# Attention with the keys on the partitions: no transposes, no row maximum, a range check behind a branch

## The chip, the cores and the metric

The kernel runs on one core of one Trainium2 chip. PE is its matmul engine, an array of 128 rows by 128 columns; DVE is the vector engine, ACT the scalar engine (here exp and tanh), POOL a general engine. PSUM is the memory that the PE writes. The metric is the device time of one execution in microseconds (us). Ratios are the mean time of one kernel's fast runs over that of the other's fast runs of the same rounds, so they are not quite the ratio of the medians that I quote.

One caution holds for all ratios of the experiments: in their rounds the kernel before ran mostly at two levels, near 4247 us (granted clock 0.985) and near 4267 to 4270 us (0.980 to 0.981), with a few runs between, all counted as fast. This widens the intervals to plus or minus 0.3 to 0.4%. The variants themselves repeat within 4 us, so I compare the variants' own medians, and read from the trace where the microseconds lie. The changed kernel was not run again on the chips of the experiments, and the two levels lie 20 us apart, so a difference of up to some 20 us alone proves nothing without its line in the trace.

## The reference, cut to what matters

Eight images of 512 channels and 32 x 32 pixels go through GroupNorm, a C2f-style block with two attention bottlenecks, and a residual add, all in float32. One bottleneck is a 3x3 convolution, the attention below (4 heads of 64 channels, 1024 pixels), and a 1x1 convolution ("m2") with silu and a residual. So the attention runs sixteen times.

```python
def bot_attention(x, qkv_w, rw, rh):
    b, c, h, w = x.shape
    hw = h * w                                        # 1024
    qkv = conv2d(x, qkv_w, 0).reshape(b, 3, HEADS, HD, hw)
    q, k, v = (qkv[:, 0], qkv[:, 1], qkv[:, 2])
    r = (rw + rh).reshape(1, HEADS, HD, hw)
    logits = jnp.einsum('bhdi,bhdj->bhij', q, k + r) * HD ** (-0.5)
    a = jax.nn.softmax(logits, axis=-1)
    out = jnp.einsum('bhij,bhdj->bhdi', a, v)
    return out.reshape(b, c, h, w)
```

## The kernel before

Channels lie on the partitions, pixels along the free axis. A pair of heads (128 channels) is worked on together: head 0 has rows 0 to 63 of the PE, head 1 rows 64 to 127. For 128 queries at a time:

```python
# logits of 128 queries: a PSUM tile for each head
ls = [ps_big.tile([P, NH, HALF], F32, tag="big", name="l_ps") for _ in range(2)]
for half in range(NH):
    for hd in range(2):
        r = slice(hd * HD, (hd + 1) * HD)
        nc.tensor.matmul(ls[hd][:, half, :], q[r, c, i0 : i0 + P], kr[r, c, ts(half, HALF)], ...)
for hd in range(2):
    nc.vector.tensor_reduce(nm, flat, AX.X, ALU.max, negate=True)        # row maximum
    nc.scalar.activation(e, flat, AF.Exp, bias=nm, accum_out=sums[:, ic, hd : hd + 1])
...
# transposes, so that the keys come to the partitions
for j in range(4):
    nc.tensor.transpose(tp[:, j, :], es[hd][:, ts(g + j, P)], ident)
...                                   # tp is copied to pts by DVE or ACT
# the reciprocal of the row sums is brought to the free axis by a product with ident
nc.vector.reciprocal(ri, sums)
nc.gpsimd.tensor_copy(rb, ri.unsqueeze(3).to_broadcast([P, NIC, 2, HD]))
nc.tensor.matmul(ps[:, 1, ts(ic, P)], rb[:, ic]..., ident, ...)
# the product with v: the heads on two halves of the PE's columns
nc.tensor.matmul(ps[hd * HD : (hd + 1) * HD, 0, :], vT[:, j, o : o + HD], pts[hd][:, j, :], ...)
```

Of the kernel before, what the change touches and what calls it, by code (L numbers as in the profile page):

```python
"""GroupNorm -> C2f-style conv block with two attention bottlenecks -> residual add.

Layout: channels on the partitions, the 1024 pixels of one image along the free axis. All of the
weights stay in SBUF; one image at a time goes through the whole block without touching HBM in
between. Everything is float32.

Attention, for a pair of heads (128 channels) and 128 queries at a time: logits with the queries on
the partitions (the two heads use the two halves of the PE rows), the row maximum on VectorE, exp
with its row sum on ScalarE, transposes on the PE, and the product with v^T for 256 queries (the two
heads use the two halves of the PE columns). The division by the row sum follows that product.  # L10

silu(y) = h * (1 + tanh(h)) with h = y / 2, which keeps Exp and Tanh in one activation table.
"""

# [1 line left out]

# [7 lines left out]
F32 = mybir.dt.float32  # L24
AF = mybir.ActivationFunctionType
ALU = mybir.AluOpType
AX = mybir.AxisListType
PSUM = bass.MemoryType.PSUM

# [3 lines left out]
GROUP = 16  # channels per GroupNorm group  # L33
HD = 64


@with_exitstack
def kernel(
    ctx: ExitStack,
    tc: tile.TileContext,  # L40
    x: bass.AP,        # (B, C1, HW)
    cv1_w: bass.AP,    # (C1, 2C)           input channel first
    cv1_bn: bass.AP,   # (2C, 4)
    cv2_w: bass.AP,    # (4C, C2)
    cv2_bn: bass.AP,   # (C2, 4)
    m_cv1_w: bass.AP,  # (N, C, 9, C)       input channel, tap, output channel
    m_cv1_bn: bass.AP,  # (N, C, 4)
    m_qkv_w: bass.AP,  # (N, C, 3C)
    m_rw: bass.AP,     # (N, C, F)
    m_rh: bass.AP,     # (N, C, F)  # L50
    m_cv2_w: bass.AP,  # (N, C, C)
    m_cv2_bn: bass.AP,  # (N, C, 4)
    out: bass.AP,      # (B, C2, HW)
# [6 lines left out]
    NX = C1 // P         # channel chunks of x  # L60
    NM = C // P          # channel chunks (= head pairs) of a bottleneck
    NO = C2 // P
    NJ = HW // P         # key chunks
    HALF = 512           # pixels of one matmul
    NH = HW // HALF
    ROWS = HALF // F
    IB = 256             # queries of one product with v
    NIB = HW // IB
    NIC = IB // P

    const = ctx.enter_context(tc.tile_pool(name="const", bufs=1))
    act = ctx.enter_context(tc.tile_pool(name="act", bufs=1))
    small = ctx.enter_context(tc.tile_pool(name="small", bufs=4))
    ps_big = ctx.enter_context(tc.tile_pool(name="ps_big", bufs=2, space=PSUM))
    ps_tr = ctx.enter_context(tc.tile_pool(name="ps_tr", bufs=2, space=PSUM))
    ps_av = ctx.enter_context(tc.tile_pool(name="ps_av", bufs=2, space=PSUM))

# [1 line left out]
    def load_x(b, c):  # L79
        xt = act.tile([P, HW], F32, tag="x", name=f"x_{b}_{c}", bufs=5)  # L80
        nc.sync.dma_start(xt, x[b, ts(c, P), :])
        return xt

    xs = [load_x(0, c) for c in range(NX)]

# [34 lines left out]
    ident = const.tile([P, P], F32, name="ident")  # L120
    make_identity(nc, ident)
    # gmat averages over the channels of a group and gives each of them the result.
# [14 lines left out]
    # y1 and y2 are kept with a border of zeros, which the 3x3 convolutions read.  # L137
# [10 lines left out]
    # BatchNorm as y/2 = sh * conv + bh: sh = g / sqrt(v + eps) / 2, bh = b / 2 - m * sh  # L148
# [16 lines left out]
    def silu_parts(ps, k):  # L165
        """h = y / 2 and tanh(h), of one PSUM bank; k names the BatchNorm chunk."""
        h = act.tile([P, HALF], F32, tag="h", name="h", bufs=2)
        t = act.tile([P, HALF], F32, tag="t", name="t", bufs=2)
        nc.vector.tensor_scalar(h, ps, sh[:, k : k + 1], bh[:, k : k + 1], ALU.mult, ALU.add)  # L169
        nc.scalar.activation(t, h, AF.Tanh)  # L170
        return h, t

    def silu(dst, ps, k):
        h, t = silu_parts(ps, k)
        if len(dst.shape) == 3:
            h, t = img(h), img(t)
        nc.vector.scalar_tensor_tensor(dst, t, 1.0, h, ALU.add, ALU.mult)

    def conv1x1(w_of, rhs_of, nk):
        """[P, NH, HALF] in PSUM: sum over nk chunks, both halves per weight."""  # L180
        ps = ps_big.tile([P, NH, HALF], F32, tag="big", name="ps")
        for k in range(nk):
            for half in range(NH):
                nc.tensor.matmul(  # L184
                    ps[:, half, :], w_of(k), rhs_of(k, half), start=(k == 0), stop=(k == nk - 1)
                )
        return ps

# [1 line left out]
    def gn_stats(mv, c, xt):  # L190
        st = small.tile([P, NH, 6], F32, tag="st", name="st")
        for half in range(NH):
            nc.vector.bn_stats(st[:, half, :], xt[:, ts(half, HALF)])
        nc.vector.bn_aggr(mv[:, c, :], st.rearrange("p a b -> p (a b)"))

    def gn_mean(mv):
        """Group means; mv's variances become those about the group's mean."""
        ps = ps_av.tile([P, NX], F32, tag="av", name="gm_ps")
        nc.tensor.matmul(ps, gmat, mv[:, :, 0], start=True, stop=True)
        gm = small.tile([P, NX], F32, tag="gm", name="gm")  # L200
        dev = small.tile([P, NX], F32, tag="dev", name="dev")
        nc.vector.tensor_copy(gm, ps)
        nc.vector.tensor_tensor(dev, mv[:, :, 0], gm, ALU.subtract)
        nc.vector.tensor_tensor(dev, dev, dev, ALU.mult)
        nc.vector.tensor_tensor(dev, dev, mv[:, :, 1], ALU.add)
        return gm, dev

    def gn_apply(gm, dev, xts):
        ps = ps_av.tile([P, NX], F32, tag="av", name="gv_ps")
        nc.tensor.matmul(ps, gmat, dev, start=True, stop=True)  # L210
        gr = small.tile([P, NX], F32, tag="gr", name="gr")
        nc.vector.tensor_scalar(gr, ps, GN_EPS, None, ALU.add)
        nc.gpsimd.tensor_tensor(gr, gr, mhalf[:, :NX], ALU.pow)
        xn = []
        for half in range(NH):
            t = act.tile([P, NX, HALF], F32, tag="pt", name="xn", bufs=3)
            for c in range(NX):
                nc.vector.tensor_scalar(  # L218
                    t[:, c, :], xts[c][:, ts(half, HALF)],
                    gm[:, c : c + 1], gr[:, c : c + 1], ALU.subtract, ALU.mult,  # L220
                )
            xn.append(t)
        return xn

# [1 line left out]
    def attention(n, z):  # L226
        q = act.tile([P, NM, HW], F32, tag="q", name="q")
        kr = act.tile([P, NM, HW], F32, tag="k", name="kr")
        vT = act.tile([P, NJ, C], F32, tag="v", name="vT")

        def project(which, c):
            o = which * C + c * P
            return conv1x1(
                lambda k: qkv_sb[:, n, k, o : o + P], lambda k, half: z[:, k, ts(half, HALF)], NM
            )

        def project_qk(c):
            ps = project(0, c)
            for half in range(NH):
                nc.scalar.activation(q[:, c, ts(half, HALF)], ps[:, half, :], AF.Copy, scale=HD**-0.5)  # L240
            ps = project(1, c)
            for half in range(NH):
                dst = img(kr[:, c, ts(half, HALF)])
                rw = rw_sb[:, n, c, :].unsqueeze(1).to_broadcast([P, ROWS, F])
                rh = rh_sb[:, n, c, ts(half, ROWS)].unsqueeze(2).to_broadcast([P, ROWS, F])
                nc.vector.tensor_tensor(dst, img(ps[:, half, :]), rw, ALU.add)  # L246
                nc.vector.tensor_tensor(dst, dst, rh, ALU.add)  # L247

        project_qk(0)
        per = NH * HALF // C  # L250
        for j0 in range(0, NJ, per):
            ps = ps_big.tile([P, per, C], F32, tag="big", name="v_ps")
            for j in range(per):
                for k in range(NM):
                    nc.tensor.matmul(  # L255
                        ps[:, j, :], z[:, k, ts(j0 + j, P)], qkv_sb[:, n, k, 2 * C : 3 * C],
                        start=(k == 0), stop=(k == NM - 1),
                    )
            for g in range(0, per, per // NH):
                nc.scalar.copy(vT[:, j0 + g : j0 + g + per // NH, :], ps[:, g : g + per // NH, :])  # L260
# [219 lines left out]
```

## Time and profile before

| | before |
|---|---|
| median time, 4 runs | 4267.16 us (4266.83 to 4267.4) |
| PE busy | 4025.7 us, 94% |
| attention with m2, mean per image, first and second bottleneck | 133.2 and 136.6 us |
| PE waits of the 3x3 convolutions on DVE | 10.0 us in all |

The prediction below shows the page's main lines. Four rows of the costliest groups are added here. A row reads: line, engine, operation, output and inputs with their sizes, number of records (a pair such as `64*128` is the part of the PE's array that is used, rows by columns); then the busy time in us and the mean of one in ns; then the idle time of the engine before them and what ended it.

```profile
L375 PE MATMUL c_ps<-ypad,m_sb 128*128 128x512 f32 x2304 | 994.8, 593 | 10.0 <-DVE ypad L398 10.0
...
L290 ACT ACTIVATE e<-l_ps,nm 128x1024 f32<-128x1024 f32 x512 | 571.7, 1117 | 629.7 <-DVE nm L288 551.0
L288 DVE TENSOR_REDUCE nm<-l_ps 128x1 f32<-128x1024 f32 x512 | 603.3, 1219 | 358.9 <-PE l_ps L280 358.9
...
L306 DVE COPY pt<-tp 128x512 f32<-128x512 f32 x512 | 351.1, 686 | 228.5 <-PE tp L303 221.2
```

### The profile page before, as it was taken

The numbers are of one execution on the slowest core, as the hardware profiler recorded it, in microseconds if no ns is written. First come the engines' busy times: TensorE is split into PE (matmuls) and PEld (weight loads), VectorE is DVE, ScalarE is ACT, GpSimd is POOL, SyncE is SP. The second block draws the span as 40 slices with busy tenths as digits, with TensorE's granted clock in tenths as the row PEclk, the third lists the DMA queues.
The fourth block names the chain that finished last, engine by engine and source line by source line (L and its number), as shares of the span: only waits on it lengthen the run. The fifth ranks groups of instructions, "written<-read, shape, count | busy, mean of one in ns | idle before, by whom it ended". The sixth has DMA issues, their size and how long they took to land.

```text
span 4268.1 us, 38190 instructions
## 1 busy us (share of the span) xinstructions
PE 4025.7 (94%) x15904; PEld 2044.4 (48%) x15904; DVE 1618.2 (38%) x2252; ACT 1156.4 (27%) x2049; POOL 108.5 (3%) x243
## 2 busy tenths in 40 slices
PE   7999999999999999999999999999999999999998
PEld 3545545445454544545445454454544445444454
DVE  2433424334243442434424244242442424424243
ACT  0323303233042330423204132041420414204142
POOL 1000000000000000000000000000000000000000
PEclk9999999999999999999999999999999999999999
DMA  3000000000000000000100001000010000100000
GB/s 120 1 1 1 17 24 1 1 1 20 20 1 1 1 20 20 1 1 1 30 10 1 1 1 30 10 1 1 1 30 10 1 0 1 35 0 1 1 1 20
DMA packets 14700, 46.12 MB, mean 11 GB/s; under 512 B 3264, under 2 KB 3776, under 8 KB 14016
## 3 DMA queue, kind: packets, MB, share of 16 engines
q1 hardware_dynamic: 4608, 16.78, 1.6%
q0 software_dynamic: 5632, 16.82, 1.0%
q10 hardware_dynamic: 4288, 10.09, 0.6%
q8 instruction: 125, 2.05, 0.2%
q14 instruction: 47, 0.39, 0.0%
HBM read 26.90 MB, written 16.78 MB: 10 GB/s over the span
## 4 chain that ended last, share of the span: by engine, by line
PE 86%; DVE 6%; ACT 4%; issue 3%; DMA 0%; POOL 0%; ACTq 0%; SPq 0%; POOLq 0%; DVEq 0%
PE c_ps L375 23%; PE ps L184 22%; PE l_ps L280 18%; PE av_ps L326 11%; PE tp L303 10%; ACT e L290 4%; DVE nm L288 4%; PE v_ps L255 3%; DVE kr L246 0%; DVE kr L247 0%; DVE h L169 0%; DMA x<-in_x_dram 0%; DVE t L393 0%; DVE t L420 0%; ACT pt L308 0%
## 5 line engine op out<-in xcount | busy, mean ns | idle before, releaser
L375 PE MATMUL c_ps<-ypad,m_sb 128*128 128x512 f32 x2304 | 994.8, 593 | 10.0 <-DVE ypad L398 10.0
L280 PE MATMUL l_ps<-kr,q 64*128 64x512 f32 x2048 | 857.3, 659 | 146.0 <-ACT e L290 146.0
L290 ACT ACTIVATE e<-l_ps,nm 128x1024 f32<-128x1024 f32 x512 | 571.7, 1117 | 629.7 <-DVE nm L288 551.0
L288 DVE TENSOR_REDUCE nm<-l_ps 128x1 f32<-128x1024 f32 x512 | 603.3, 1219 | 358.9 <-PE l_ps L280 358.9
L375 PEld LDWEIGHTS c_ps<-ypad,m_sb 128*128 128x128 f32 x2304 | 434.1, 189 | 569.3 <-issue 546.1
L303 PEld LDWEIGHTS tp<-ident,e 128*128 128x128 f32 x4096 | 448.5, 143 | 419.2 <-issue 211.9
L170 ACT ACTIVATE t<-h 128x512 f32<-128x512 f32 x256 | 161.3, 630 | 1692.9 <-DVE h L169 1682.9
L303 PE MATMUL tp<-ident,e 128*128 128x128 f32 x4096 | 595.7, 284 | 1.4
L326 PE MATMUL av_ps<-pt,vT 128*64 128x256 f32 x4096 | 473.1, 382 | 0.0
L280 PEld LDWEIGHTS l_ps<-kr,q 64*128 64x128 f32 x2048 | 264.3, 193 | 372.5 <-ACT e L290 183.7
L306 DVE COPY pt<-tp 128x512 f32<-128x512 f32 x512 | 351.1, 686 | 228.5 <-PE tp L303 221.2
L326 PEld LDWEIGHTS av_ps<-pt,vT 128*64 128x64 f32 x4096 | 291.7, 137 | 210.8 <-issue 87.6
L169 DVE TENSOR_SCALAR h<-c_ps,sh,bh 128x512 f32<-128x512 f32 x64 | 48.9, 806 | 887.2 <-PE c_ps L375 887.2
L308 ACT COPY pt<-tp 128x512 f32<-128x512 f32 x512 | 297.3, 581 | 295.5 <-PE tp L303 295.5
L169 DVE TENSOR_SCALAR h<-ps,sh,bh 128x512 f32<-128x512 f32 x192 | 148.0, 805 | 338.4 <-PE ps L184 338.4
L184 PE MATMUL ps<-xn,cv_sb 128*128 128x512 f32 x512 | 240.9, 634 | 15.6 <-DVE xn L218 15.6
L184 PE MATMUL ps<-z,qkv_sb 128*128 128x512 f32 x512 | 227.7, 595 | 0.0
L184 PE MATMUL ps<-ypad,cv_sb 128*128 128x512 f32 x512 | 225.9, 592 | 0.0
L332 DVE TENSOR_TENSOR ao<-av_ps,rs 128x256 f32<-128x256 f32 x128 | 54.2, 424 | 347.2 <-ACT rs L331 347.2
L184 PEld LDWEIGHTS ps<-xn,cv_sb 128*128 128x128 f32 x512 | 103.8, 205 | 146.8 <-issue 125.6
L184 PEld LDWEIGHTS ps<-ypad,cv_sb 128*128 128x128 f32 x512 | 96.6, 189 | 124.0 <-issue 124.0
L184 PEld LDWEIGHTS ps<-z,qkv_sb 128*128 128x128 f32 x512 | 95.8, 190 | 119.9 <-issue 94.9
(62 smaller groups left out, 1652.2 us busy)
## 6 DMA issues: line engine op xcount, KB each, us to landing
x<-in_x_dram SPq DMA_DIRECT2D x32, 512.0 KB, 4.3
out_dram<-t POOLq DMA_DIRECT2D x64, 256.0 KB, 2.5
m_sb<-in_m_cv_w_dram ACTq DMA_DIRECT2D x2, 2304.0 KB, 13.7
cv_sb<-in_cv_w_dram ACTq DMA_DIRECT2D x1, 2048.0 KB, 14.4
qkv_sb<-in_m_qkv_w_dram ACTq DMA_DIRECT2D x2, 768.0 KB, 15.7
cv_sb<-in_cv_w_dram ACTq DMA_DIRECT2D x1, 1024.0 KB, 9.7
m_sb<-in_m_cv_w_dram ACTq DMA_DIRECT2D x2, 256.0 KB, 10.5
bnp<-in_cv_bn_dram POOLq DMA_DIRECT2D x8, 2.0 KB, 6.7
```

What stands on the lines that cost most here:

```text
L169: nc.vector.tensor_scalar(h, ps, sh[:, k : k + 1], bh[:, k : k + 1], ALU.mult, ALU.add)
L170: nc.scalar.activation(t, h, AF.Tanh)
L184: nc.tensor.matmul(ps[:, half, :], w_of(k), rhs_of(k, half), start=(k == 0), stop=(k == nk - 1))
L255: nc.tensor.matmul(ps[:, j, :], z[:, k, ts(j0 + j, P)], qkv_sb[:, n, k, 2 * C : 3 * C], start=(k == 0), stop=(k == NM - 1),)
L280: nc.tensor.matmul(ls[hd][:, half, :], q[r, c, i0 : i0 + P], kr[r, c, ts(half, HALF)], start=True, stop=True,)
L288: nc.vector.tensor_reduce(nm, flat, AX.X, ALU.max, negate=True)
L290: nc.scalar.activation(e, flat, AF.Exp, bias=nm, accum_out=sums[:, ic, hd : hd + 1])
L303: nc.tensor.transpose(tp[:, j, :], es[hd][:, ts(g + j, P)], ident)
L306: nc.vector.tensor_copy(dst, tp)
L308: nc.scalar.copy(dst, tp)
L326: nc.tensor.matmul(ps[hd * HD : (hd + 1) * HD, 0, :], vT[:, j, o : o + HD], pts[hd][:, j, :], start=(j == 0), stop=(j == NJ - 1),)
L375: nc.tensor.matmul(ps[:, half, :], m1_sb[:, n, k, tap, ts(oc, P)], yi[:, k, r0 : r0 + ROWS, dx : dx + F], start=(k == 0 and tap == 0), sto ...
```

## The change

The intent: if the logits are computed with the keys on the partitions, exp's output is already the operand of the product with v. The transposes and their copies go. A maximum over the keys would then run across partitions, so it is dropped as well. The sum over the keys becomes an addition on DVE over the eight key chunks, and one product with a matrix of ones, which also spreads the sum over the 64 channels of a head. Without the maximum, exp may overflow. The kernel therefore keeps the largest and the smallest sum, tests them at the end, and runs a general path (the old scheme) if a sum is outside 1e-18 to 1e18.

The diff, cut to its core (the layout of stages, loads and the general path is left out):

```diff
-ls = [ps_big.tile([P, NH, HALF], F32, tag="big", name="l_ps") for _ in range(2)]
-...                    # queries on the partitions, maximum, exp with bias, transposes
+for i, (_, j) in enumerate(pair):                  # two key chunks: one burst
+    ps = ps_big.tile([P, 2, HALF], F32, tag="big", name="l_ps")
+    for hd in range(2):
+        r = slice(hd * HD, (hd + 1) * HD)
+        nc.tensor.matmul(ps[:, hd, :], kr[r, c, ts(j, P)], q[r, c, ts(half, HALF)], ...)
+    nc.scalar.activation(pt[:, i], ps, AF.Exp, scale=SCALE)
+...                    # acc = sum of the pt, on DVE
+nc.tensor.matmul(avs[g][hd * HD : (hd + 1) * HD, :], vT[:, j, o : o + HD], pt[:, i, hd, :], ...)
+...
+def divide(g):
+    for hd in range(2):
+        nc.tensor.matmul(ps[hd * HD : (hd + 1) * HD, :], ones, acc[:, hd, :], ...)
+    nc.vector.tensor_scalar(rs, ps, 1.0, None, ALU.mult, ALU.max, accum_out=smax[:, i : i + 1])
+    nc.vector.tensor_reduce(smin[:, i : i + 1], rs, AX.X, ALU.min)
+    nc.vector.reciprocal(rs, rs)
+    nc.vector.tensor_tensor(dst, dst, rs, ALU.mult)
@@ m2
-for oc in range(NM):  ps = conv1x1(...); silu of both halves
+pss = [ps_big.tile([P, NH, HALF], F32, tag="big", name="m2_ps") for _ in range(NM)]
+for half in range(NH):              # the half whose division is done first goes first
+    for oc in range(NM):
+        for k in range(NM):
+            nc.tensor.matmul(pss[oc][:, half, :], ...)
@@ end
+held = nc.values_load(n_good[0:1, 0:1])            # partitions whose sums are in range
+with tc.If(held < P):
+    ...                                            # the general path for all images
```

## The prediction

> **What bounds the kernel now.** I read the page from the top: busy time of the engines, then the chain that ended last, then the costliest groups.
>
> ```profile
> PE 4025.7 (94%) x15904; PEld 2044.4 (48%) x15904; DVE 1618.2 (38%) x2252; ACT 1156.4 (27%) x2049; POOL 108.5 (3%) x243
> ...
> PE 86%; DVE 6%; ACT 4%; issue 3%; DMA 0%; POOL 0%; ACTq 0%; SPq 0%; POOLq 0%; DVEq 0%
> PE c_ps L375 23%; PE ps L184 22%; PE l_ps L280 18%; PE av_ps L326 11%; PE tp L303 10%; ACT e L290 4%; DVE nm L288 4%; PE v_ps L255 3%; DVE kr L246 0%; DVE kr L247 0%; DVE h L169 0%; DMA x<-in_x_dram 0%; DVE t L393 0%; DVE t L420 0%; ACT pt L308 0%
> ...
> L280 PE MATMUL l_ps<-kr,q 64*128 64x512 f32 x2048 | 857.3, 659 | 146.0 <-ACT e L290 146.0
> ...
> L303 PE MATMUL tp<-ident,e 128*128 128x128 f32 x4096 | 595.7, 284 | 1.4
> L326 PE MATMUL av_ps<-pt,vT 128*64 128x256 f32 x4096 | 473.1, 382 | 0.0
> ```
>
> The kernel is bound by the PE: 86% of the chain. About 47% of the chain is attention (l_ps, av_ps, tp, and the waits on e and nm), and only that is changed. The l_ps row also shows that a large part of its time is not arithmetic. A float32 matmul is two records here, so 2048 records are 1024 matmuls, and 857 us / 1024 = 0.84 us each: one after the other, although each uses only 64 of the 128 rows. The av_ps row, whose two heads lie on two halves of the columns, is 473 us / 2048 = 0.23 us per matmul of half the length: those do run two at a time. The timeline shows both cases for l_ps (start, length, line, records):
>
> ```profile
> 141.14 3.49 PE L280 MATMUL l_ps<-kr,q 64*128 64x512 f32 x8
> ```
> ```profile
> 1777.66 1.09 PE L303 MATMUL tp<-ident,e 128*128 128x128 f32 x8
> 1778.60 0.61 PE L319 MATMUL av_ps<-ident,rb 128*128 128x128 f32 x4
> 1780.34 1.12 PE L280 MATMUL l_ps<-kr,q 64*128 64x512 f32 x2 [1.13 <-ACT e L290]
> 1781.39 1.09 PE L303 MATMUL tp<-ident,e 128*128 128x128 f32 x8
> 1782.41 1.98 PE L280 MATMUL l_ps<-kr,q 64*128 64x512 f32 x6
> 1784.33 3.67 PE L326 MATMUL av_ps<-pt,vT 128*64 128x256 f32 x32
> 1787.93 1.09 PE L303 MATMUL tp<-ident,e 128*128 128x128 f32 x8
> 1788.95 1.12 PE L280 MATMUL l_ps<-kr,q 64*128 64x512 f32 x2
> 1790.01 0.66 PE L303 MATMUL tp<-ident,e 128*128 128x128 f32 x4
> 1790.59 1.12 PE L280 MATMUL l_ps<-kr,q 64*128 64x512 f32 x2
> 1791.64 0.66 PE L303 MATMUL tp<-ident,e 128*128 128x128 f32 x4
> 1792.23 1.13 PE L280 MATMUL l_ps<-kr,q 64*128 64x512 f32 x4
> ```
>
> At 141 us eight records (four matmuls, scheduled head 0, head 0, head 1, head 1) take 3.42 us, 0.853 each: serial. At 1792.23 four records (two matmuls, of different heads) take no longer than the two records at 1790.59: concurrent. A lone one of 0.853 us costs 1.05 to the start of the next group, so 0.19 us goes with each change between half-array and whole-array forms; the 32 av_ps records give the same, 3.60 - 16 x 0.213 = 0.19. One period, from av_ps to av_ps, is 15.63 us: logits 6.1, transposes 4.1, av 3.6, the row-sum transposes 0.6, and one wait of 1.1 for ACT. There are eight per attention and sixteen attentions.
>
> **What the Trainium skill says.** "TensorE: Matmul & The Clock Gate", Part 3 (packing small matmuls): tiles of different row or column groups run concurrently, and weights are pulled ahead only where row groups differ. The trace agrees (the two cases above). "TensorEngine Tiling (Array Packing)", Key Properties: changing the tiling mode drains the array; here 0.19 us. "VectorE: DVE Perf Modes", the fixed hardware budget: Reciprocal is an iterated divide with a repeat count of 8. The trace has only the 128x4 reciprocal, 176 ns against 148 to 161 ns for other 128x4 operations: 5 to 8 cycles per element, so it fits but doesn't settle it. The TensorE page's Part 1: after an idle window the clock is halved until the array has been busy. The trace shows 0.67 granted between 359 and 385 us, after PE waits at the start of an attention; most attentions have 0.99.
>
> **The change part by part.** With keys on the partitions exp's output is already the operand of the product with v. Removed: all 4096 transposes, 1024 evictions pt on DVE and ACT (351 + 297 us), 512 row maxima (603 us) and the wait chain logits-maximum-exp, the row-sum transposes, and POOL's broadcast. Added: per attention 28 DVE adds of 128x1024 (acc), and four divisions (a column sum by a matmul with ones, then on DVE a copy with maximum, a minimum, a reciprocal of 128x512, a product). The order of the changed program's instructions shows the two heads' logits always adjacent, in bursts of two key chunks (four matmuls) alternating with four av matmuls, now 512 wide.
>
> PE, per attention: a pair of logits matmuls is 0.853 us, a pair of av matmuls 2 x 0.427 = 0.853. Logits: a first burst of 4 pairs 3.41 + 0.19 = 3.60, then 14 bursts of 2 pairs, 1.71 + 0.19 = 1.90 each, 26.6. av: 14 x 1.90 = 26.6 and a last one of 3.60. Four sums with ones, 0.853 each, 3.4 (same column form as av, so no new switch). Sum 63.8 us.
>
> ACT: 32 exps of 128x1024 at about 1.06 (tanh 128x512 is 0.63; 512 elements more, as exp's 1.117 implies) plus four copies of 0.58: 36 us. Hidden.
>
> DVE: an add of 128x512 takes 0.692 us, of 1024 then 0.692 + 512/0.96 ns = 1.225; times 28, 34.3. A division: copy 0.8 (as h from PSUM, 0.805), minimum 0.69, reciprocal 0.146 + 512 x 8 / 0.96 ns = 4.4 (estimate from the VectorE page's 8), product 0.69: 6.6, times four 26.3. Sum 60.6, close under the PE. Per group of eight key chunks DVE needs 7 x 1.225 + 6.6 = 15.2 us and the PE 4 x 3.79 + 0.85 = 16.0; three pt buffers of two chunks leave slack for the reciprocal's 4.4, so inside the loop PE should not wait.
>
> It waits at the end, where the last group has no successor. After the third sum DVE has 0.8 + 0.69 + 4.4 + 0.69 + 4 x 1.225 = 11.5 us until the last acc is whole; the PE has 1.9 + 1.9 + 1.9 + 1.7 + 1.9 = 9.3: a wait of 2.2. After the fourth sum the division takes 6.7 with latencies; six of the eight m2 matmuls (5.3) don't need it, so 1.4 to 1.5 more, 0.65 in the second bottleneck, where a cv2 matmul is pulled in. In the first bottleneck the next 3x3 convolution then waits on DVE, which begins silu only after the reciprocal: counting DVE's order (h, h, t, ypad, ...) against two m2 matmuls and two first ones I get 1.3 + 2.65 = 3.9; before it was 0.45 + 0.80 = 1.25.
>
> Sum, from first logits to end of m2 (7.0 with its switch): first bottleneck 63.8 + 2.2 + 7.0 + 1.5 + 3.9 = 78.4 against before 133.2 (mean of eight) + 1.25; second 63.8 + 2.2 + 7.0 + 0.65 = 73.7 against 136.6. Gain per image 56.0 + 62.9 = 119, times eight 952 us. The end check lies behind cv2 except for the last load of a count and the branch; I allow 5 us. I allow 10 us for a halved clock after the end-of-attention waits. The sums' logarithms, computed from the reference's inputs, lie between 5.3 and 12.4, far inside 1e-18 to 1e18, so the general path isn't taken. 4267 - 952 + 15 = 3330 us.
>
> **Rivals.** (1) DVE becomes the bound. For it: 60.6 against 63.8 us per attention, with the reciprocal unmeasured. If its division is 1.5 us longer, DVE sets the pace of the loop and the tail grows: about 3 us per attention, 3380. Against: at 5 cycles per element it is 1.6 us shorter, the tail waits nearly vanish, about 3275. (2) The row-tiled logits don't overlap pair after pair, since the trace never shows two pairs in sequence, only one pair followed by one single. If all 32 pairs ran serially, 27 us per attention or 437 us: 3770. The form x6 in 1.92 us (a pair, then a single, with no gap) speaks against it. (3) The clock: short waits at every attention's end could halve it for one to five windows (the trace has halved stretches of 3.4 to 17 us by the granted clock). One window of 3.4 us costs 1.7; for all sixteen 27, and the longest ones 130. (4) The switch of form costs nothing when it is only half-array to half-array: 28 x 0.19 x 16 = 85 us less, 3245.
>
> **Range and chances.** Terms (1), (3) and (4) give about 3245 to 3420; (2) and the general path are outside, at a few per cent. Predicted 3330, range 3245 to 3420. Faster by over 2%: 0.98. A result within 2% would need the general path or both engines serialised.
>
> **What would show it.** Right: tp, nm and rb rows gone; l_ps about 0.43 us of busy PE time per matmul (437 us in all, half of before); acc adds near 1.225 us; the reciprocal near 4.4; PE waits on DVE only near s_ps, the second half of m2 and the first c3 matmuls; DVE at about 85% inside attention. Wrong: l_ps waiting for ACT or DVE in the loop (buffers), av_ps waiting for exp, l_ps busy time near 870 us (no overlap), or a granted clock under 0.95.

## More of the kernel before

The loops name the heads in turn, but in the built program the first logits of an attention stand in the order head 0, head 0, head 1, head 1, as the prediction says.

The convolution row (c_ps) is the yardstick: the change does not touch it, so I read any growth of its busy time as a slower clock, and any growth of its wait comes from what lies ahead of it. The row maximum (nm) takes 603 us of DVE, but only the part that the PE waits for costs anything.

## The result, and the profile after

| | before | after |
|---|---|---|
| median time, 4 runs each | 4267.16 us | 3306.32 us (3304.56 to 3307.59) |
| ratio | | 0.7747 (0.7736 to 0.7758) |
| attention with m2, first bottleneck | 133.2 us | 72.5 us |
| attention with m2, second bottleneck | 136.6 us | 72.8 us |

The kernel is faster by 960.8 us. The output is correct, and the general path was not taken. First the page's busy line and the shares of the chain, after the change:

```profile
PE 3168.1 (96%) x9506; PEld 1303.5 (39%) x9506; DVE 1490.6 (45%) x1746; ACT 763.3 (23%) x961; POOL 57.3 (2%) x116
...
PE 77%; issue 13%; DVE 8%; DMA 1%; POOL 1%; ACT 0%; SPq 0%; DVEq 0%; POOLq 0%
```

The two spans differ by 962.5 us (4268.1 against 3305.6). The PE's busy time fell by 857.6 us (4025.7 to 3168.1), so its idle time fell by the remaining 104.9. The PE is still the engine that sets the time. The yardstick's row, the rows that took the place of logits, transposes, maximum and copies, and the reciprocal:

```profile
L432 PE MATMUL c_ps<-ypad,m_sb 128*128 128x512 f32 x2304 | 1013.8, 601 | 28.1 <-DVE ypad L462 27.1
...
L301 ACT ACTIVATE pt<-l_ps 128x1024 f32<-128x1024 f32 x512 | 494.5, 1022 | 387.0 <-PE l_ps L297 387.0
...
L307 DVE TENSOR_TENSOR acc<-acc,pt 128x1024 f32<-128x1024 f32 x384 | 467.0, 1216 | 132.3 <-ACT pt L301 109.9
L297 PE MATMUL l_ps<-q,kr 64*128 64x512 f32 x2048 | 504.4, 613 | 0.0
L318 PE MATMUL av_ps<-pt,vT 128*64 128x512 f32 x2048 | 492.4, 604 | 0.0
...
L339 DVE RECIPROCAL rs<-rs 128x512 f32<-128x512 f32 x64 | 214.6, 3353 | 2.2
```

The logits have the same 2048 records as before, but 504.4 us in place of 857.3, and no wait in place of 146.0. Neither logits nor products with v wait for anything inside the loop. What the PE waits for at the ends of the attentions stands in the view of waits (engine, tile and line; what it waited for; us in total, times, longest):

```profile
PE c_ps L432 <- DVE ypad L462: 27.1, 16, 2.4
...
PE s_ps L330 <- DVE acc L307: 17.4, 16, 1.1
...
PE m_ps L450 <- DVE ao L341: 2.9, 8, 0.4
```

And the PE's timeline at the start of one attention, and at its end (start, length, line, records):

```profile
1118.05 3.71 PE L297 MATMUL l_ps<-q,kr 64*128 64x512 f32 x16
1121.68 1.94 PE L318 MATMUL av_ps<-pt,vT 128*64 128x512 f32 x8
1123.55 1.99 PE L297 MATMUL l_ps<-q,kr 64*128 64x512 f32 x8
1125.47 1.94 PE L318 MATMUL av_ps<-pt,vT 128*64 128x512 f32 x8
...
1181.99 1.08 PE L330 MATMUL s_ps<-acc,ones 128*64 128x512 f32 x4 [1.09 <-DVE acc L307]
```

Read the starts: the first burst of logits takes 1121.68 - 1118.05 = 3.63 us, a later one 1125.47 - 1123.55 = 1.92 us, with four matmuls (eight records) in it. A serial float32 logits matmul took 0.853 us in the kernel before, so four of them in 1.92 us run two at a time. The last sum waits 1.09 us for the DVE additions.

### The profile page after: what moved, and what is told of

It is laid out like the page before. It is cut to its first block, busy times and chain, and to the rows that moved or that the text cites. A ratio compares the mean times of both kernels' runs of the same rounds, so it can differ in the third digit from the quotient of the medians.

```text
span 3305.6 us, 23035 instructions
## 1 busy us (share of the span) xinstructions
PE 3168.1 (96%) x9506; PEld 1303.5 (39%) x9506; DVE 1490.6 (45%) x1746; ACT 763.3 (23%) x961; POOL 57.3 (2%) x116
## 4 chain that ended last, share of the span: by engine, by line
PE 77%; issue 13%; DVE 8%; DMA 1%; POOL 1%; ACT 0%; SPq 0%; DVEq 0%; POOLq 0%
PE c_ps L432 26%; PE ps L200 24%; PE l_ps L297 11%; PE av_ps L318 9%; DVE acc L307 3%; PE v_ps L268 3%; DVE rs L339 2%; PE m_ps L450 2%; PE s_ps L330 1%; DMA x<-in_x_dram 1%; DVE h L183 1%; DVE smin L338 0%; DVE rs L335 0%; ACT pt L301 0%; DVE t L457 0%
## 5 line engine op out<-in xcount | busy, mean ns | idle before, releaser
L432 PE MATMUL c_ps<-ypad,m_sb 128*128 128x512 f32 x2304 | 1013.8, 601 | 28.1 <-DVE ypad L462 27.1
L301 ACT ACTIVATE pt<-l_ps 128x1024 f32<-128x1024 f32 x512 | 494.5, 1022 | 387.0 <-PE l_ps L297 387.0
L307 DVE TENSOR_TENSOR acc<-acc,pt 128x1024 f32<-128x1024 f32 x384 | 467.0, 1216 | 132.3 <-ACT pt L301 109.9
L297 PE MATMUL l_ps<-q,kr 64*128 64x512 f32 x2048 | 504.4, 613 | 0.0
L318 PE MATMUL av_ps<-pt,vT 128*64 128x512 f32 x2048 | 492.4, 604 | 0.0
L297 PEld LDWEIGHTS l_ps<-q,kr 64*128 64x128 f32 x2048 | 177.6, 186 | 322.0 <-issue 314.5
L318 PEld LDWEIGHTS av_ps<-pt,vT 128*64 128x64 f32 x2048 | 125.6, 136 | 337.3 <-issue 264.1
L339 DVE RECIPROCAL rs<-rs 128x512 f32<-128x512 f32 x64 | 214.6, 3353 | 2.2
L304 DVE TENSOR_TENSOR acc<-pt 128x1024 f32<-128x1024 f32 x64 | 78.4, 1225 | 107.8 <-ACT pt L301 107.8
L450 PE MATMUL m_ps<-ao,m_sb 128*128 128x512 f32 x256 | 117.6, 602 | 2.9 <-DVE ao L341 2.9
L200 PE MATMUL ps<-y,cv_sb 128*128 128x512 f32 x256 | 116.4, 592 | 0.0
```

Source lines behind the costliest of these rows:

```text
L200: nc.tensor.matmul(ps[:, half, :], w_of(k), rhs_of(k, half), start=(k == 0), stop=(k == nk - 1))
L297: nc.tensor.matmul(ps[:, hd, :], kr[r, c, ts(j, P)], q[r, c, ts(half, HALF)], start=True, stop=True,)
L301: nc.scalar.activation(pt[:, i], ps, AF.Exp, scale=SCALE)
L304: nc.vector.tensor_tensor(accs[g], pt[:, 0], pt[:, 1], ALU.add)
L307: nc.vector.tensor_tensor(accs[g], accs[g], pt[:, i], ALU.add)
L318: nc.tensor.matmul(avs[g][hd * HD : (hd + 1) * HD, :], vT[:, j, o : o + HD], pt[:, i, hd, :], start=(j == 0), stop=(j == NJ - 1),)
```

## The experiments

All were correct but one, which was wrong. In the order of the questions: does the gain come from two heads running at once; what does a change of form cost (from the logits, which use half of the PE's rows, to the products with v, which use half of its columns, or back); how much room has DVE; where do the end waits come from; what was the maximum worth; and what is left to win.

### Heads in series

```diff
-for i, (_, j) in enumerate(pair):
-    for hd in range(2): matmul(ps_i[:, hd, :], ...)     # order 0, 1, 0, 1
+for hd in range(2):
+    for i, (_, j) in enumerate(pair): matmul(lps[i][:, hd, :], ...)   # order 0, 0, 1, 1
```

> The changed kernel with the four logits matmuls of a burst in the order head 0, head 0, head 1, head 1 instead of 0, 1, 0, 1. If two heads run at once because they use different rows: at best the middle two still overlap, so a burst needs 3 x 0.853 instead of 2 x 0.853 us; 16 bursts, 16 attentions: 218 us more, 3525 us. If nothing overlaps any more, 437 us more, 3743. Rival (the logits are not the PE's limit, their pairing doesn't matter): 3306.

Measured: 3334.54 us, only 28 us more. The overlap was expected to vanish, and it did not:

```profile
1124.99 2.84 PE L297 MATMUL l_ps<-q,kr 64*128 64x512 f32 x10
1128.10 1.99 PE L297 MATMUL l_ps<-q,kr 64*128 64x512 f32 x6 [0.27 <-ACT pt L302]
1130.02 1.94 PE L319 MATMUL av_ps<-pt,vT 128*64 128x512 f32 x8
1131.88 1.99 PE L297 MATMUL l_ps<-q,kr 64*128 64x512 f32 x8
```

The burst at 1131.88 still holds eight records in 1.93 us (the next group starts at 1133.81). The built program has the order head 0, head 0, head 1, head 1 there. The single records can be told apart by their semaphores: the third matmul (head 1) bears the counter update that ends its tile, the second (head 0) a wait on ACT at its weight load. By them the third matmul began at 1131.90, 0.01 us after the first, and the second only at 1132.85, when the rows of head 0 were free. So the PE starts the other head's matmul ahead of one that stands before it and needs busy rows.

The first burst shows the limit of this. Its ten records from 1124.99 are four matmuls two at a time, and then two lone records at 1126.81 and 1127.24: a fifth matmul, of head 0, by itself. The next one in order is another of head 0 that waits for ACT's exp to free its tile (0.27 us in the line at 1128.10), and head 1's matmul behind it did not start until that wait was over. A compiler that had swapped the order beforehand would have swapped it in this burst too. The PE's instruction stream has the order head 0, head 0, head 1, head 1 as well. So the swap is the PE's own doing. The first burst takes 5.03 us in place of 3.63, 1.40 x 16 = 22 us; the rest of the 28 is more waiting for the last sums (29.8 in place of 17.4 us) against a less often halved clock (c_ps busy 1000.7 in place of 1013.8).

So this experiment did not do what it was made for, and the worth of the overlap stayed open.

### Twice the switches

The same matmuls in bursts of one key chunk: logits, product with v, logits, product with v.

```diff
-logits(pairs[i]);  times_v(pairs[i - 1])                 # bursts of two key chunks
+for half_pair in range(PAIR):                            # bursts of one
+    logits(pairs[i], half_pair);  times_v(pairs[i - 1], half_pair)
```

> The changed kernel with bursts of one key chunk (two matmuls) instead of two, so about 60 instead of 30 changes of form per attention; work and buffers are the same. At 0.19 us a change: 30 to 32 x 0.19 x 16 = 91 to 97 us more, about 3400. Rival (a change between the two half-array forms costs nothing): 3306.

Measured: 3369.29 us, 63 us more, about two thirds of the 91 to 97 expected. The trace gives the cost of a change of form directly:

```profile
1180.01 1.13 PE L298 MATMUL l_ps<-q,kr 64*128 64x512 f32 x4
1181.07 1.08 PE L321 MATMUL av_ps<-pt,vT 128*64 128x512 f32 x4
1182.08 1.13 PE L298 MATMUL l_ps<-q,kr 64*128 64x512 f32 x4
```

One key chunk takes 2.07 us here and 3.79 / 2 = 1.895 us in the changed kernel (1127.34 - 1123.55 = 3.79 from logits to logits). The difference, 0.175 us, is one change of form more per chunk. The built programs have 59 and 29 changes per attention; 30 more make 30 x 16 x 0.175 = 84 us. The waits for the last sums (11.4 in place of 17.4 us) and of the convolutions (20.5 in place of 27.1) gave 13 of them back, since a slower PE leaves DVE more time, and a less often halved clock another 6 (c_ps busy 1008.0 in place of 1013.8). That leaves 65, against 63 measured.

### Heads apart

This is the test that the first experiment failed to be. The two matmuls of head 0 and the two of head 1 are separated by products with v, in the same number of changes of form as in the run before.

```diff
-for hd in range(2): matmul(ps[:, hd, :], kr[r, c, ts(j, P)], ...)       # both heads, one key chunk
+r = slice(i * HD, (i + 1) * HD)                                         # one head, both key chunks
+for n_, (_, j) in enumerate(pair): matmul(ps[:, n_, :], kr[r, c, ts(j, P)], ...)
```

> The run with the heads in series still overlapped them, so it did not measure what the overlap is worth. Here the two logits matmuls of head 0 and the two of head 1 are kept apart by the two matmuls with v of the step before, in the same number of changes of form as the run with twice the switches (3369 us), whose neighbours are heads of both halves. Theory A (the gain of the changed kernel needs both heads in flight in one burst): 30 of the 32 pairs of an attention take 2 x 0.853 us in place of 0.853, so 30 x 0.853 = 25.6 us per attention, 16 x 25.6 = 410 us more than 3369: about 3780 us, with bursts of 1.7 + 0.2 for each head. Rival B (the overlap is worth little, the gain came from the removed transposes): within 50 us of 3369 us.

Measured: 3811.96 us, 443 us more than with twice the switches and 506 us more than the changed kernel; theory A had 410 more.

```profile
1149.43 1.98 PE L297 MATMUL l_ps<-q,kr 64*128 64x512 f32 x4
1151.35 1.08 PE L320 MATMUL av_ps<-pt,vT 128*64 128x512 f32 x4
1152.36 1.98 PE L297 MATMUL l_ps<-q,kr 64*128 64x512 f32 x4
```

A burst with two matmuls of one head takes 1151.35 - 1149.43 = 1.92 us, where two matmuls of two heads took 1181.07 - 1180.01 = 1.06. The busy time of the logits is 978.2 us, against 569.4 with twice the switches. Theory A holds: running the two heads at once is worth more than 400 us in the changed kernel, by far more than the switches. Even so this run is faster than the kernel before (ratio 0.8953, 0.8919 to 0.8987): the overlap is somewhat less than half of the 961 us.

### A PSUM tile for each head

Why, then, were the logits of the kernel before so often serial? Inside its loop mostly because other work stands between them, as in the run with heads apart: of its 1024 logits matmuls 320 stand alone in the built program, next to transposes or products, and 384 in groups of three, of which two can pair. Only at the start of an attention, at 141 us in the prediction's timeline, do the heads stand next to each other in the order 0, 0, 1, 1, and those were serial too, although order alone does not do it. In the kernel before each head has its own PSUM tile, so a wait stands in the queue between head 0's matmuls and head 1's. This run gives the changed kernel such tiles.

```diff
-for i, (_, j) in enumerate(pair):
-    ps = ps_big.tile([P, 2, HALF], ...)                  # both heads of one key chunk
-    for hd in range(2): matmul(ps[:, hd, :], ...)
+for hd in range(2):
+    ps = ps_big.tile([P, PAIR, HALF], ...)               # one head, two key chunks
+    for i, (_, j) in enumerate(pair): matmul(ps[:, i, :], ...)
```

> In the kernel before each head's logits had a PSUM tile of its own, so a wait stood in the PE's queue between head 0's two matmuls and head 1's; there the logits were largely serial. Here the changed kernel gets the same: a tile for each head (two key chunks in it), head 0's two matmuls, then a wait, then head 1's two. In the loop that wait is for an exp that is over by then (three tiles, about 1.1 us of exp under 1.9 us of matmuls with v); in the first burst of an attention it may still be open. Theory A (only a wait that is still open holds the other head's rows back): bursts in the loop stay at 1.92 us and only the first burst grows, by up to 1.7 us, so 3306 to 3335 us. Rival B (any wait between the heads makes them serial): about 410 us more, near 3720 us.

Measured: 3343.98 us, 38 us more; a little above theory A's range and far from B.

```profile
1131.10 5.08 PE L297 MATMUL l_ps<-q,kr 64*128 64x512 f32 x16
1136.10 1.94 PE L318 MATMUL av_ps<-pt,vT 128*64 128x512 f32 x8
1137.97 1.99 PE L297 MATMUL l_ps<-q,kr 64*128 64x512 f32 x8
```

In the loop, where the tile is free when its turn comes, the burst stays at 1.92 us (the next group starts at 1139.89). In the first burst it grows to 5.00 us: 1.37 x 16 = 22 us. The rest is in the waits for the sums (20.4 in place of 17.4 us), in m2's (9.8 in place of 2.9) and in the products with v (498.2 in place of 492.4 us busy). So it is not the tile or the wait as such that keeps the heads apart, but a wait that is still open. The kernel before shows the same at 141 us:

```profile
141.25 1.29 DVE L246 TENSOR_TENSOR kr<-ps,rw_sb 128x512 f32<-128x512 f32 x2 [11.29 <-PE ps L184]
```

DVE reads the projections from PSUM until 142.54 us (141.25 + 1.29), and in the built program head 1's first matmul stands behind a wait for DVE. That matmul began at 142.68, while head 0's second was still running. In the second burst, at 146 us, the wait is for the exp of the tile's last contents: it ended at 147.24, and head 1 began at 147.29.

### One and two spare reciprocals

A reciprocal whose result nobody uses is added to each of the first two of an attention's four divisions, once or twice. The last division, on which the end waits, is left alone.

```diff
     nc.vector.tensor_reduce(smin[:, i : i + 1], rs, AX.X, ALU.min)
+    for _ in range(1 if g < 2 else 0):          # in the second run: 2 if g < 2
+        spare = act.tile([P, HALF], F32, tag="spare", name="spare")
+        nc.vector.reciprocal(spare, rs)
     nc.vector.reciprocal(rs, rs)
```

> One more reciprocal of 128x512, thrown away, in the first two of the four divisions of each attention. If the PE sets the pace and DVE has about 2 us of slack per group (13.95 of 16.0), no wait inside the loop; but DVE comes 1.3 us later to each of two divisions and the last column sum waits 2.6 us more: at most 42 us, 3306 to 3348. Rival (DVE already sets the pace): 2 x 3.35 x 16 = 107 us, 3413.

> Two more reciprocals in each of the first two divisions: DVE then needs 20.7 us per group against the PE's 16.0 and must set the pace: estimate 13.4 less about 4 of slack, times 16: 150 us more, 3455, with PE waits on acc or pt inside the loop. If DVE had far more slack than I think: under 3350.

Measured: 3340.78 us with one (34 more) and 3426.57 us with two (120 more, where 150 were expected). One spare in each of two divisions is 2 x 3.34 = 6.7 us of DVE per attention, 107 us in all, of which 34 arrived; the second adds another 107, of which 86 arrived. So DVE has room for most of the first of the two, as the sum in the prediction said (DVE close under the PE), and then it sets the pace. The waits of the PE are where they should be: for the sums, 44.8 us with one and 112.9 us with two, against 17.4. With two there are 48 such waits, three per attention, so they now lie inside the loop too:

```profile
PE s_ps L330 <- DVE acc L307: 112.9, 48, 3.6
```

### No reciprocal

The reciprocal is a multiplication with a constant. The result was wrong (relative error 0.17), as it had to be.

```diff
-nc.vector.reciprocal(rs, rs)
+nc.vector.tensor_scalar(rs, rs, 1e-12, None, ALU.mult)
```

> Wrong result on purpose: each reciprocal is replaced by a multiplication by 1e-12 (about 0.54 us instead of 3.35). Theory A (as predicted: all waits at the end of an attention, the convolution's too, come from the reciprocal): the waits of 17.4 + 2.9 + 27.1 us and the 19 us of halved clock nearly vanish, 3240. Theory B (the convolution's wait comes from the order of the silu pieces and from m2's two halves sharing a PSUM tile): only the first two go, about 20 us, 3285.

Measured: 3262.03 us, 44 us less, between the two theories. The waits for the last sums and of m2 are gone (17.4 + 2.9 us), and the convolutions' busy time falls from 1013.8 to 997.9 us, 16 us, by a less often halved clock (the changed kernel's trace has six stretches of 6.8 us at half the clock in its convolutions, this one two of 3.4 us); m2's own busy time is 3.5 us shorter. That is 40 of the 44. But the convolutions' wait stays:

```profile
PE c_ps L432 <- DVE ypad L462: 27.8, 15, 2.1
```

It was 27.1 us with the reciprocal. So the prediction's reason for this wait, that DVE begins silu only after the reciprocal, does not hold.

### m2 by halves

In the changed kernel a PSUM tile of m2 holds both halves of the pixels for one chunk of output channels. The first half's matmuls come first, but silu cannot read them before the tile's last matmul, of the second half. Here each tile holds one half for both chunks.

```diff
-pss = [... for _ in range(NM)];  order: half, oc, k;  matmul(pss[oc][:, half, :], ...)
-silu in the order half, oc
+pss = [... for _ in range(NH)];  order: half, k, oc;  matmul(pss[half][:, oc, :], ...)
+silu in the order oc, half
```

> The changed kernel with m2's PSUM tiles by half of the pixels instead of by channel chunk, and silu in the order of channel chunks, so the first chunk of the convolution's input is ready first. The reciprocal stays. Theory B: the convolution's wait of 27.1 us falls under 10 and the halved clock behind it (19 us) goes: about 3265. Theory A: 3306, within 10.

Measured: 3270.39 us, 36 us less, as theory B said.

```profile
PE c_ps L432 <- DVE h L183: 6.1, 8, 0.8
PE c_ps L432 <- DVE ypad L462: 2.2, 8, 0.3
```

The convolutions now wait 8.3 us in place of 28.1 (27.1 of them in the line above), and their busy time is 996.1 us in place of 1013.8. The two are 38 us; m2's wait grew by 3.4. The reciprocal is as long as before. So this wait came from m2's tiles and the order of silu, which this run changes together. The traces show both. In the changed kernel DVE waits 1.22 us for m2's matmuls before its first silu piece, at 211.54 us; with the tiles cut, this piece starts at 210.18, before the second half's last matmuls (211.54). And the convolution's second, shorter wait (0.57 us) ends with the other half of the first chunk, which the old order put third. No run separates their shares. Nor is it shown that this wait alone halved the clock: with the heads in series and without the reciprocal the wait was as long (29.2 and 27.8 us), and c_ps was busy for only 1000.7 and 997.9 us.

### No end check

```diff
-ends, good, g_ps, n_good; held = nc.values_load(...); with tc.If(held < P): general path
```

> The changed kernel without the count, its load, the branch and the general path (the maxima and minima stay): my estimate for all this is 4 to 5 us, so 3301. Rival (the large program behind the branch costs instruction fetches throughout): more than 10 us.

Measured: 3301.6 us, 4.7 us less, as expected. The trace agrees: from the issue of the last output to the end of the span it is 3305.6 - 3293.4 = 12.2 us in the changed kernel, and 7.9 us in the kernel before. The difference, 4.3 us, is the check and the branch. (In this run the same stretch takes 8.4 us, 3.8 less.)

### The kernel before without the row maximum

```diff
-nc.vector.tensor_reduce(nm, flat, AX.X, ALU.max, negate=True)
-nc.scalar.activation(e, flat, AF.Exp, bias=nm, accum_out=sums[:, ic, hd : hd + 1])
+nc.scalar.activation(e, flat, AF.Exp, accum_out=sums[:, ic, hd : hd + 1])
```

> The kernel before without its row maximum (no bias in exp), nothing else changed. If the maximum cost only waits, as the PE-bound account says: the wait of 1.14 us per period, 128 periods, 146 us, and a few us at each attention's start, less 0.19 us for changes of form: 4080 to 4150. So most of the 961 us would belong to the transposes and to the pairing of the heads. Rival (the chain logits, maximum, exp is the limit and the PE only looks busy): under 3950.

Measured: 4166.8 us against 4251.31 us for the kernel before in the same rounds; ratio 0.9788 (0.9752 to 0.9824). That is about 2%, 85 us by the medians, or 100 against the level of 4267, of the 961; the interval lies on both sides of 2%, so the verdict at that bar is unclear, and the expected 4080 to 4150 us was missed by 17. The logits' waits fall from 146.0 to 20.3 us, and yet their busy time stays (862.5 us against 857.3), and the PE is now 97% busy: 4047.7 us in place of 4025.7, although the granted clock rose from 0.980 to 0.992. Why its work took longer was not followed. The maximum's 603 us of DVE were mostly hidden. The gain of the whole change lies in what the PE itself does no longer: transposes, and logits one after the other.

### Short tail

m2 by halves, and besides the reciprocal straight from PSUM; the range check reads the reciprocals (largest and smallest) after it, for the last divisions only after m2 has been served.

```diff
-tensor_scalar(rs, ps, 1.0, ..., accum_out=smax);  tensor_reduce(smin, rs, min);  reciprocal(rs, rs)
+nc.vector.reciprocal(rs, ps)
+late.append(in_range)         # max and min of rs, put behind what the PE waits for
```

> m2_by_halves, and the reciprocal straight from PSUM with the range check on the reciprocals, after the product, for the last two groups put off to after m2. The last column sum should no longer wait (17.4 us), the second half of m2 neither: about 3245, the best of all.

Measured: 3260.24 us, 46 us less than the changed kernel and 10 less than with m2 by halves alone; 15 us were missing to the expectation. The wait for the last sums fell only to 10.5 us (17.4), m2's vanished (6.3), the convolutions' stayed at 8.2, and the granted clock fell from 0.990 to 0.987. Why the sums still wait was not followed.

### Longer bursts

The short tail with bursts of four key chunks where the buffers allow it (four pt buffers, one rs buffer): 14 changes of form fewer per attention.

```diff
-logits(p[i]); times_v(p[i - 1])
+logits(p[2m - 1]); logits(p[2m]); times_v(p[2m - 2]); times_v(p[2m - 1])
```

> The short-tail kernel (3260 us) with bursts of four key chunks in place of two where it can (four pt buffers, one rs buffer): 14 changes of form fewer per attention, 224 in all. Theory A (the PE sets the pace and each change costs 0.13 to 0.19 us): 29 to 43 us less, 3217 to 3231 us. Rival B (ACT's exps, the three PSUM buffers of the logits or the four pt buffers then make the PE wait inside the bursts): 3260 us or more, with waits of l_ps or av_ps on ACT in the trace.

Measured: 3234.14 us, 26 us less than the short tail and 72 us less than the changed kernel (ratio to the kernel before 0.7596, 0.7568 to 0.7625), 3 us above theory A's range. This is the fastest version.

```profile
1100.58 3.70 PE L298 MATMUL l_ps<-q,kr 64*128 64x512 f32 x16
1104.21 3.65 PE L319 MATMUL av_ps<-pt,vT 128*64 128x512 f32 x16
1107.80 3.70 PE L298 MATMUL l_ps<-q,kr 64*128 64x512 f32 x16
```

Four key chunks take 7.22 us in place of 2 x 3.79 = 7.58: two changes of form fewer, 0.18 us each, which makes 224 x 0.18 = 40 us. Part is given back: the waits for the last sums are 22.7 us in place of 10.5, since DVE gets its last chunks later against the PE. 40 - 12 = 28, against 26 measured. No logits and no product with v waited for ACT, so rival B fell.

## Why the prediction was right

Predicted were 3330 us in a range of 3245 to 3420; measured 3306.32. Term by term:

| term | predicted | measured |
|---|---|---|
| first burst; later burst; pair of bursts | 3.60; 1.90; 3.80 us | 3.63; 1.92; 3.79 us |
| acc addition, 128x1024 | 1.225 us | 1.216 to 1.225 us |
| exp, 128x1024 | 1.06 us | 1.022 us |
| logits, PE busy in all | 437 us | 504.4 us |
| reciprocal, 128x512 | 4.4 us | 3.353 us |
| wait for the last sums, each | 2.2 us | 17.4 / 16 = 1.1 us |
| wait of m2, first bottleneck, each | 1.5 us | 2.9 / 8 = 0.36 us |
| wait of the convolution, each | 3.9 us | 27.1 / 8 = 3.4 us |
| first bottleneck with the convolution's wait | 78.4 us | 72.5 + 3.4 = 75.9 us |
| second bottleneck | 73.7 us | 72.8 us |
| halved clock | 10 us | 1013.8 - 994.8 = 19 us |
| end check | 5 us | 4.3 us (4.7 by the run without it) |

**The mechanism held.** The PE stayed the bound, transposes and row-sum transposes went with all their time, and the logits ran two at a time. Heads apart shows that the overlap was needed: without it, at an equal number of changes of form, the kernel takes 443 us more, which was rival 2. Twice the switches and longer bursts put a change of form at 0.175 to 0.18 us, against the 0.19 that the prediction read from the kernel before; rival 4, in which it costs nothing, fell. Rival 1, DVE as the bound, fell too, but not by much: one spare reciprocal in two of the four divisions already costs 34 us.

**The term that was mis-sized is the reciprocal.** The prediction took eight cycles per element from the repeat count in the Trainium skill ("VectorE: DVE Perf Modes", the fixed hardware budget) and got 4.4 us. It is 3.353 us, 1.05 less, and this is why the waits at the end of an attention were 1.1 us shorter each. Per image the two bottlenecks gain 133.2 + 1.25 - 75.9 = 58.55 and 136.6 - 72.8 = 63.8 us in place of the predicted 56.0 and 62.9, which makes 8 x 122.35 = 979 in place of 952. The halved clock took 9 us of these 27 back. 4267 - 979 + 19 + 4 = 3311, and 5 us stay unexplained.

**Two of the prediction's reasons were wrong, though neither cost it the number.** The convolution's wait was put on DVE's order behind the reciprocal, and came out near its size, 3.4 in place of 3.9 us. But without a reciprocal it stays at 27.8 us in all, and with m2's tiles cut by halves and silu reordered it falls to 8.3: those two were the cause, in shares that no run separates. And the prediction named the order, head 0, head 0, head 1, head 1, beside the serial logits at 141 us of the kernel before, and took its mean of 0.84 us per matmul for one after the other throughout. Heads in series has that order and overlaps all the same, and a tile per head overlaps except in its first burst. At 141 us a wait for DVE in front of head 1's first matmul was open until 142.54 us; I did not remove it in the kernel before itself, so its worth is not measured. In the loop, transposes and products stood between the heads.

**Where the 961 us came from.** Of the PE's time 857.6 us were work: 595.7 of transposes, 82.5 of row-sum transposes, and 857.3 - 504.4 = 352.9 of logits, less 66.6 for the sums by ones, 19.3 more for the products with v, and 19 of slower clock in the convolutions. (These add up to 926; busy times of neighbouring groups overlap at their borders, and the kernel before has many more borders.) A part of the logits and transposes is clock: the trace of the kernel before has the clock at half for 3.4 or 17.1 us at the start of 13 of its 16 attentions, 99 us in all, and the changed kernel has no such stretch in an attention. The other 104.9 us were waits: 146.0 of the logits, less 17.4, 2.9 and 17.1 of new waits for sums, m2 and convolutions, and 4.3 for the end check: 104.3.

## What to carry to other kernels

Choose the layout in which a stage's output is the next stage's operand, and count what the PE is spared rather than what the other engines are: removing 603 us of row maximum from the old layout gave 2%, and the rest of the change another 20%. In these runs two half-array matmuls overlapped when neither other matmuls nor a wait that was still open stood between them, so give what is to run together one PSUM tile (38 us here), and keep what is read at different times, as m2's two halves, in different ones. After such a change look at the ends of the stages: the end waits, the halved clock near them and the changes of form were still worth 72 us here.

## What the Trainium skill lacked or had wrong

- "TensorE: Matmul & The Clock Gate", Part 3, says that matmuls keep program order in start and end ("strict FIFO, no reordering"). With the heads in series the third matmul of a burst (other rows) began at 1131.90 us and the second, in the same rows as the first, at 1132.85; the burst still took 1.93 us for four matmuls of 0.853. The records were told apart by their semaphores, and the compiled instruction stream has the second before the third.
- Nor has that page a second condition for the overlap of row groups that the runs show: no open wait between them. A tile per head kept bursts of 1.92 us in the loop, and took 5.00 in place of 3.63 us in the first burst; in the kernel before head 1 began at 142.68 us, after a wait that was open until 142.54.
- "TensorEngine Tiling (Array Packing)", Key Properties, says that a change of tiling mode drains the array, without a figure: 0.175 to 0.18 us per change between the row form and the column form here.
- "VectorE: DVE Perf Modes", the fixed hardware budget, gives the reciprocal a repeat count of 8, and no time. Measured were 3353 ns for 128x512. An addition grows from 692 to 1216 ns with 512 more elements, 1.02 ns each; the reciprocal grows from 176 ns for 128x4 (in the kernel before) to 3353 ns with 508 more elements, 6.25 ns each, so six times as much and not eight.
